# Moving delta*u*B of a selective scan from VectorE to ScalarE and TensorE, one state at a time

## Chip, core and metric

The kernel runs on one core of a Trainium2 chip. The metric is the device time of one launch in microseconds (us). Before the change it is 28022.95 us, the median of three runs (27987.81 to 28037.46). The core has five engines that run side by side, each with its own queue of instructions: TensorE (PE, matmuls and transposes, with its weight loads shown apart as PEld), VectorE (DVE), ScalarE (ACT), GpSimd (POOL) and SyncE (SP, which issues most DMAs). PE's results go to PSUM, a small memory from which DVE and ACT read; everything else lies in the large on-chip memory, SBUF. [...]

## What is computed

An image batch of four 128x128 images with 128 channels goes through two residual layers, each after a group norm. Layer 0 is a deformable convolution: offsets from a 3x3 convolution, a bilinear gather at nine taps, a depthwise and a pointwise convolution. Layer 1 treats each image row, 128 pixels, as a sequence of tokens t, and runs two Mamba blocks over it. The part that the change touches is the selective scan of a block:

```
delta  = softplus(dt @ dtw + dtb)
deltaA = exp(delta[t,d] * A[d,n])
deltaBu = (delta * u)[t,d] * B[t,n]
h = deltaA * h + deltaBu          # along t, for each channel d and state n
y[t,d] = sum_n h[t,d,n] * C[t,n] + u * D
out = (y * silu(res)) @ ow
```

There are 256 channels d (`NC` = 2 chunks of 128 partitions), 16 states n (`NS`), and two blocks (`NL`). Everything is fp32.

## The kernel before, in words

Work of layer 1 comes in jobs. A job is one block `l` of one group of `SR` = 4 image rows, 512 tokens (`TB`); there are 128 groups and two blocks, so 256 jobs. A job has two parts. `pre` (lines 484 to 551) makes what the scan needs, with channels on the partitions and tokens along the free axis: u (`pu` matmuls, L501, then silu, L508), the gate g (L513, L518), the small projection `dbl` with dt, B and C (L521, L524), delta (`pdt` matmuls L534, the softplus as Abs, Exp, Identity, Ln on ACT, L538 to L546, and the joins on DVE, L547 to L549), and du = delta*u (L550). B and C are written to DRAM (`bcd`, L526), so that they can be read back with every partition holding the same row.

`main` (lines 553 to 631) goes over the states in rounds of `NQ` = 2. In a round, SP loads the two B rows and the two C rows, each spread over 128 partitions (L570). ACT sets the first column of every row in the decay tile to zero (L575), so that one long scan restarts at each row, and writes the decays exp(delta*A) beside it (L580), into one of `NDA` = 3 fixed tiles `da`. DVE multiplies du by B into `hs` (L584), scans over 2048 elements in one instruction with the result in `da` (L591), and multiplies by C (L595). PE then transposes the sixteen 128x128 blocks and adds them in the two PSUM banks of `y` (`add_transposed`, L128, called at L603), where the sum over n is made. At the end of a job the result is gated (L606), transposed back (L611), projected (L616, L623, L625) and either becomes the next block's input h or goes out.

Layer 0 of an image: POOL gathers table entries with indirect DMAs (L364) into the four `gt` buffers, DVE weighs them (`gw`, L382), PE transposes them into `p` (L128 again), ACT copies that out (L396), and PE makes the convolution sums `acc` (L415). `prep` computes locations and weights eight rows ahead.

Layer 1 of image b and layer 0 of image b+1 are written interleaved, by counting: one step of layer 0 (a unit of eight gathers) after a share of a round of layer 1 (the loop at lines 656 to 669). In the program, `pre` of the next job is written before `main` of the present one. The order on each engine is not that of the program text, though: a scheduler of the framework places instructions by its own estimate of when each is ready, with earlier text first among those that are ready, and adds the semaphores. A tile's tag has a number of buffers (`bufs`); a new tile of a tag waits until the last user of the oldest one is done.

Four pools share PSUM before the change: `ps` (layer 0's transposes and small matmuls, 2 buffers of a bank), `psa` (`acc`, 2), `ps1` (everything in `pre` and at the end of a job, 2) and `psy` (`y`, one buffer of two banks).

Of the kernel before, what the change touches and what calls it, by code (L numbers as in the profile page):

```python
# [10 lines left out]
F32 = mybir.dt.float32  # L11
# [6 lines left out]
P = 128  # L18
# [45 lines left out]
def block_kernel(ctx: ExitStack, tc: tile.TileContext, a: dict, out: bass.AP):  # L64
# [27 lines left out]
    ps = ctx.enter_context(tc.tile_pool(name="l0ps", bufs=2, space=PSUM))  # L92
# [3 lines left out]
    ps1 = ctx.enter_context(tc.tile_pool(name="l1ps", bufs=2, space=PSUM))  # L96
# [29 lines left out]
    def add_transposed(o, v, start, stop):  # L126

        nc.tensor.matmul(o, v, ident, is_transpose=True, start=start, stop=stop, skip_group_check=True)  # L128
# [355 lines left out]
    def pre(st, l):  # L484
# [40 lines left out]
        bcd = pd.tile([2 * NS, TB], F32, tag="bcd", name=f"bcd_{nm}")  # L525
        nc.sync.dma_start(bcd, dbl[DTR + 1 : XP, :])  # L526
# [3 lines left out]
        du = p2.tile([P, NC, TB], F32, tag="du", name=f"du_{nm}", bufs=2)  # L530
# [20 lines left out]
        st.update(u=u, g=g, delta=de, du=du, bcd=bcd)  # L551

    def main(st, l):
# [11 lines left out]
        for q in range(NS // NQ):  # L565
            bc = []
            for w in range(2):
                t = p2.tile([P, NQ, TB], F32, tag=f"bc{w}", name=f"bc{w}_{nm}_{q}", bufs=2)
                n0 = w * NS + q * NQ
                nc.sync.dma_start(t, st["bcd"][n0 : n0 + NQ, :].partition_broadcast(P))  # L570
                bc.append(t)
            da = das[n_da[0] % NDA]
            n_da[0] += 1

            nc.scalar.copy(da.rearrange("p c n s t -> p (c n s) t")[:, :, 0], zero)  # L575
            for c in range(NC):
                dv = st["delta"][:, c].rearrange("p (s t) -> p s t", s=SR)
                for n in range(NQ):
                    s = q * NQ + n
                    nc.scalar.activation(  # L580
                        da[:, c, n, :, 1:], dv[:, :, 1:], AF.Exp, scale=aneg[:, l, c, s : s + 1]
                    )
            hs = p2.tile([P, NC, NQ, TB], F32, tag="hs", name=f"hs_{nm}_{q}")
            nc.vector.tensor_tensor(  # L584
                hs,
                st["du"].unsqueeze(2).to_broadcast([P, NC, NQ, TB]),
                bc[0].unsqueeze(1).to_broadcast([P, NC, NQ, TB]),
                ALU.mult,
            )
            df = da.rearrange("p c n s t -> p (c n s t)")  # L590
            nc.vector.tensor_tensor_scan(  # L591
                df, df, hs.rearrange("p c n t -> p (c n t)"), 0.0, ALU.mult, ALU.add
            )
            dc = da.rearrange("p c n s t -> p c (n s t)")
            nc.vector.tensor_tensor(  # L595
                dc, dc,
                bc[1].rearrange("p n t -> p (n t)").unsqueeze(1).to_broadcast([P, NC, NQ * TB]),
                ALU.mult,
            )
            for c in range(NC):  # L600
                for n in range(NQ):
# [145 lines left out]
```

## Time and profile before

| | |
|---|---|
| median of three runs | 28022.95 us |
| the profiled execution, its own time | 28027.08 us |
| its span | 28025.3 us |
| mean granted PE clock | 0.834 |
| DVE busy | 22925.4 us |
| PE busy | 19874.5 us |
| POOL busy | 18817.1 us |
| ACT busy | 11640.4 us |
| moved by DMA | 3804.39 MB, 136 GB/s |

The page of a profile gives the busy time of each engine, a strip of the span in slices, and groups of instructions: line, engine, operation, output and inputs, count, busy time, the mean of one in ns, and how long the engine stood idle just before them with what ended that idle time. Windows give the same busy times for a stretch of the span. The timeline lists instructions with their start and duration in us. A wait is put down to what came last. Busy time of PE is modelled and somewhat too long for matmuls that follow one another closely, since these overlap; the distance from start to start is the better measure there.

### The profile page before, as it was taken

Reading aid. Unit: us, or ns where it says so; the run is one execution under the profiler, and the core shown is the slowest. Engines: PE = TensorE matmul, PEld = TensorE weight load, DVE = VectorE, ACT = ScalarE, POOL = GpSimd, SP = SyncE. Lnnn points to the kernel's source line nnn. Section 1 sums busy time; section 2 is a strip of 40 time slices with the busy share of each in tenths; the row PEclk is TensorE's granted clock in tenths of the full one; section 3 lists DMA queues with packets and bytes.
Section 4 is the critical chain, followed back from the end, with each engine's and each line's share of the span. In section 5 each row is a group of like instructions: output and inputs, shape, how many; then the busy total and the mean of one; then the engine's idle time right before and its main releaser. Section 6 shows DMA issues by size and latency. Waiting matters only on the chain. (4 is left out here: it accounts for less than half of the span.)

```text
span 28025.3 us, 292712 instructions
## 1 busy us (share of the span) xinstructions
PE 19874.5 (71%) x112196; PEld 13790.6 (49%) x112196; DVE 22925.4 (82%) x11994; ACT 11640.4 (42%) x18190; POOL 18817.1 (67%) x9222
## 2 busy tenths in 40 slices
PE   4777777777777777777777777777777755555555
PEld 3444455555555545555555555555555544434344
DVE  2232288888888898888888898888888899999999
ACT  0000144444444444444444444444444455555554
POOL 4777788888888878888888878888888800000000
PEclk7888888888888888888888888888888877667777
DMA  5363344455444444445444444444444433333333
GB/s 142 114 168 107 111 142 145 146 161 162 149 142 139 142 135 146 147 151 168 152 142 144 139 138 140 144 142 144 140 143 143 138 113 107 109 107 109 107 109 104
DMA packets 1994584, 3804.39 MB, mean 136 GB/s; under 512 B 771795, under 2 KB 1116115, under 8 KB 1993052
## 3 DMA queue, kind: packets, MB, share of 16 engines
q1 hardware_dynamic: 1550812, 2577.13, 28.6%
q0 software_dynamic: 442368, 1208.55, 13.6%
q8 instruction: 880, 14.42, 0.2%
q14 instruction: 524, 4.29, 0.0%
HBM read 3567.63 MB, written 217.05 MB: 135 GB/s over the span
## 5 line engine op out<-in xcount | busy, mean ns | idle before, releaser
L364 POOL DMA_INDIRECT gt<-table,idx x9216 | 18816.4, 2042 | 3674.8 <-issue 3042.2
L591 DVE TENSOR_TENSOR_SCAN da<-da,hs 128x2048 f32<-128x2048 f32 x2048 | 9056.4, 4422 | 498.9 <-ACT da L580 407.2
L128 PE MATMUL y<-ident,da 128*128 128x128 f32 x32768 | 5361.3, 331 | 4518.1 <-DVE da L595 4515.5
L580 ACT ACTIVATE da<-de,aneg 128x508 f32<-128x508 f32 x8192 | 5569.7, 713 | 6349.2 <-PE y L128 6151.5
L128 PEld LDWEIGHTS y<-ident,da 128*128 128x128 f32 x32768 | 4780.2, 174 | 5499.1 <-DVE da L595 3050.8
L415 PE MATMUL acc<-s,wc 128*64 128x256 f32 (+3 forms) x38400 | 6435.8, 457 | 887.3 <-ACT s L396 885.9
L382 DVE TENSOR_TENSOR gw<-gt,wt 128x1024 f32<-128x1024 f32 x2304 | 2794.9, 1219 | 3919.9 <-DMA gt<-table,idx 3268.9
L415 PEld LDWEIGHTS acc<-s,wc 128*64 128x64 f32 x38400 | 3399.3, 147 | 3237.7 <-issue 1456.8
L595 DVE TENSOR_TENSOR da<-da,bc 128x2048 f32<-128x2048 f32 x2048 | 4688.0, 2289 | 25.5
L584 DVE TENSOR_TENSOR hs<-du,bc 128x2048 f32<-128x2048 f32 x2048 | 4680.3, 2285 | 0.0
L128 PE MATMUL p<-ident,gw 128*128 128x128 f32 x18432 | 2790.5, 304 | 2015.4 <-DVE gw L382 2007.3
L128 PEld LDWEIGHTS p<-ident,gw 128*128 128x128 f32 x18432 | 2361.0, 158 | 2609.6 <-DVE gw L382 2036.7
L396 ACT COPY s<-p 128x512 f32<-128x512 f32 x1152 | 669.8, 582 | 4377.9 <-PE p L128 4370.7
L501 PE MATMUL pu<-hp,inc 128*128 128x512 f32 x4096 | 1808.3, 593 | 0.0
L580 ACT ACT_TABLE_LOAD x1019 | 1307.4, 1283 | 10.2
L501 PEld LDWEIGHTS pu<-hp,inc 128*128 128x128 f32 x4096 | 751.9, 189 | 865.1 <-issue 864.9
L508 ACT ACTIVATE u<-pu,w_cvb 128x512 f32<-128x512 f32 x512 | 324.0, 683 | 1448.5 <-PE y L561 1442.5
L611 PE MATMUL pyg<-ident,g 128*128 128x128 f32 x2048 | 366.0, 337 | 522.0 <-DVE g L606 521.9
L561 PEld LDWEIGHTS y<-ddiag,u 128*128 128x128 f32 x4096 | 585.1, 202 | 197.6 <-issue 197.6
L546 ACT ACT_TABLE_LOAD x506 | 649.2, 1283 | 9.0
L612 ACT COPY yg<-pyg 128x512 f32<-128x512 f32 x512 | 284.9, 588 | 813.3 <-PE pyg L611 813.2
L561 PE MATMUL y<-ddiag,u 128*128 128x128 f32 x4096 | 614.4, 285 | 0.0
(118 smaller groups left out, 11438.6 us busy)
## 6 DMA issues: line engine op xcount, KB each, us to landing
bc<-bcd SPq DMA_DIRECT2D x4096, 512.0 KB
gt<-table,idx POOLq DMA_INDIRECT x9216
table<-xt SPq DMA_DIRECT2D x984, 128.0 KB
xt<-in_x SPq DMA_DIRECT2D x124, 320.0 KB
xr<-in_x SPq DMA_DIRECT2D x128, 256.0 KB
x<-xo SPq DMA_DIRECT2D x128, 256.0 KB
x1t<-x SPq DMA_DIRECT2D x128, 256.0 KB
x1t_o<-x SPq DMA_DIRECT2D x128, 256.0 KB
```

Of the source, the lines that this page charges most:

```text
L128: nc.tensor.matmul(o, v, ident, is_transpose=True, start=start, stop=stop, skip_group_check=True)
L364: nc.gpsimd.indirect_dma_start(out=gt[:, v, r], out_offset=None, in_=flat, in_offset=bass.IndirectOffsetOnAxis(ap=idx[:, ri, o : o + 1], a ...
L382: nc.vector.tensor_tensor(gw.rearrange("p r s v c -> p (r s) v c"), gts[h].rearrange("p v r (s c) -> p (r s) v c", c=CG), wv.unsqueeze(3). ...
L396: nc.scalar.copy(st[:, :, 1 : W + 1], p4)
L415: nc.tensor.matmul(accs[b, j + i0][CG * g : CG * g + CG, q : q + rb - ra, :], wc[sl, v, e, :], st[p + 4 * g if p < 4 else 8][sl, ra:rb, kx ...
L501: nc.tensor.matmul(px.rearrange("p (s t) -> p s t", s=SR), inc[:, l, j, c * P : (c + 1) * P], h[:, :, j : j + P], start=(j == 0), stop=(j ...
L546: nc.scalar.activation(du[:, c], w1, AF.Ln)
L561: nc.tensor.matmul(y[:, i, c], st["u"][:, c, i * P : (i + 1) * P], ddiag[:, l, c, :], start=(i % 2 == 0 and c == 0), stop=False, skip_grou ...
L580: nc.scalar.activation(da[:, c, n, :, 1:], dv[:, :, 1:], AF.Exp, scale=aneg[:, l, c, s : s + 1])
L584: nc.vector.tensor_tensor(hs, st["du"].unsqueeze(2).to_broadcast([P, NC, NQ, TB]), bc[0].unsqueeze(1).to_broadcast([P, NC, NQ, TB]), ALU.mult,
L591: nc.vector.tensor_tensor_scan(df, df, hs.rearrange("p c n t -> p (c n t)"), 0.0, ALU.mult, ALU.add)
L595: nc.vector.tensor_tensor(dc, dc, bc[1].rearrange("p n t -> p (n t)").unsqueeze(1).to_broadcast([P, NC, NQ * TB]), ALU.mult,)
```

## The change

delta*u*B is no longer made by DVE. At the end of `pre`, PE transposes du into `ps1`, and ACT copies it to `dut`, with tokens on the partitions and channels along the free axis. B is transposed in the same way into `bt`, tokens on the partitions, one column for each state. For each state, ACT then multiplies: four copies of 128x256, one for each image row, with the state's column of `bt` as the scale that differs by partition, into `xs`. PE transposes the eight 128x128 blocks of `xs` into `px`, two PSUM banks, and the scan reads its second input there.

`main` now goes one state at a time: scans, products with C and decays cover 1024 elements for each instruction, not 2048. The decays keep three tiles, now half as large, of their own: the scan writes to `hs` (three buffers), so the zeros in the first columns are set once at the start and stay, and the copy of L575 is gone. Only C goes through DRAM (`cd`), two rows at a time into `cs`. The sixteen transposes for `y` of two states are as before.

To make room in PSUM, `ps` and `ps1` go from two buffers to one, and `psx` (px) takes two banks. `du` has one buffer where it had two. The load of `cvw` during set-up is split into one for each block.

```diff
-    ps = ctx.enter_context(tc.tile_pool(name="l0ps", bufs=2, space=PSUM))
+    ps = ctx.enter_context(tc.tile_pool(name="l0ps", bufs=1, space=PSUM))
...
-    ps1 = ctx.enter_context(tc.tile_pool(name="l1ps", bufs=2, space=PSUM))
+    ps1 = ctx.enter_context(tc.tile_pool(name="l1ps", bufs=1, space=PSUM))
+    psx = ctx.enter_context(tc.tile_pool(name="l1psx", bufs=1, space=PSUM))
...
-    cvw = loadw("cvw", [P, NL, DCONV, NC * P], pool=p2, tag="hs")
     for l in range(NL):
+        cvw = p2.tile([P, DCONV, NC * P], F32, tag="dut", name=f"w_cvw_{l}", bufs=2)
+        nc.sync.dma_start(cvw, a["cvw"][:, l])
...
-    das = [cw.tile([P, NC, NQ, SR, P], F32, name=f"da{i}") for i in range(NDA)]
-    zero = cw.tile([P, NC * NQ * SR], F32, name="zero")
-    nc.vector.memset(zero, 0.0)
+    das = [cw.tile([P, NC, SR, P], F32, name=f"da{i}") for i in range(NDA)]
+    for t in das:
+        nc.vector.memset(t, 0.0)
...
-        bcd = pd.tile([2 * NS, TB], F32, tag="bcd", name=f"bcd_{nm}")
-        nc.sync.dma_start(bcd, dbl[DTR + 1 : XP, :])
+        cd = pd.tile([NS, TB], F32, tag="cd", name=f"cd_{nm}")
+        nc.sync.dma_start(cd, dbl[DTR + 1 + NS : XP, :])
+
+        pbt = ps1.tile([P, SR, XP], F32, tag="t", name=f"pbt_{nm}")
+        for i in range(SR):
+            nc.tensor.transpose(pbt[:, i, :], dbl[:, i * P : (i + 1) * P], ident[0:XP, 0:XP])
+        bt = p2.tile([P, SR, NS], F32, tag="bt", name=f"bt_{nm}", bufs=2)
+        nc.scalar.copy(bt, pbt[:, :, DTR + 1 : DTR + 1 + NS])
...
-        du = p2.tile([P, NC, TB], F32, tag="du", name=f"du_{nm}", bufs=2)
+        du = p2.tile([P, NC, TB], F32, tag="du", name=f"du_{nm}")
...
+        dut = p2.tile([P, SR, NC * P], F32, tag="dut", name=f"dut_{nm}", bufs=2)
+        for k in range(SR // 2):
+            pt = ps1.tile([P, 2, NC, P], F32, tag="t", name=f"pdu_{nm}_{k}")
+            for i in range(2):
+                for c in range(NC):
+                    o = (2 * k + i) * P
+                    nc.tensor.transpose(pt[:, i, c, :], du[:, c, o : o + P], ident)
+            nc.scalar.copy(dut[:, 2 * k : 2 * k + 2], pt.rearrange("p s c d -> p s (c d)"))
...
-        for q in range(NS // NQ):
...
+        for n in range(NS):
+            if n % NQ == 0:
+                cs = p2.tile([P, NQ, TB], F32, tag="cs", name=f"cs_{nm}_{n}", bufs=2)
+                nc.sync.dma_start(cs, st["cd"][n : n + NQ, :].partition_broadcast(P))
             da = das[n_da[0] % NDA]
             n_da[0] += 1
-
-            nc.scalar.copy(da.rearrange("p c n s t -> p (c n s) t")[:, :, 0], zero)
             for c in range(NC):
                 dv = st["delta"][:, c].rearrange("p (s t) -> p s t", s=SR)
...
+                nc.scalar.activation(da[:, c, :, 1:], dv[:, :, 1:], AF.Exp, scale=aneg[:, l, c, n : n + 1])
+
+            xs = p2.tile([P, SR, NC * P], F32, tag="xs", name=f"xs_{nm}_{n}", bufs=2)
+            for i in range(SR):
+                nc.scalar.activation(xs[:, i], st["dut"][:, i], AF.Copy, scale=st["bt"][:, i, n : n + 1])
+            px = psx.tile([P, NC, SR, P], F32, tag="x", name=f"px_{nm}_{n}")
+            for c in range(NC):
+                for i in range(SR):
+                    nc.tensor.transpose(px[:, c, i, :], xs[:, i, c * P : (c + 1) * P], ident)
+            hs = p2.tile([P, NC, TB], F32, tag="hs", name=f"hs_{nm}_{n}", bufs=3)
+            nc.vector.tensor_tensor_scan(
+                hs.rearrange("p c t -> p (c t)"),
+                da.rearrange("p c s t -> p (c s t)"),
+                px.rearrange("p c s t -> p (c s t)"),
+                0.0, ALU.mult, ALU.add,
+            )
             nc.vector.tensor_tensor(
-                hs,
-                st["du"].unsqueeze(2).to_broadcast([P, NC, NQ, TB]),
-                bc[0].unsqueeze(1).to_broadcast([P, NC, NQ, TB]),
-                ALU.mult,
-            )
...
+                hs, hs, cs[:, n % NQ].unsqueeze(1).to_broadcast([P, NC, TB]), ALU.mult
             )
             for c in range(NC):
-                for n in range(NQ):
-                    for i in range(SR):
-                        add_transposed(y[:, i, c], da[:, c, n, i, :], False, q == NS // NQ - 1 and n == NQ - 1)
-            yield
+                for i in range(SR):
+                    add_transposed(y[:, i, c], hs[:, c, i * P : (i + 1) * P], False, n == NS - 1)
+            if n % NQ == NQ - 1:
+                yield
```

More of the change, by code (lines that the diff above doesn't have):

```diff
@@ L162, in block_kernel @@
     inw = loadw("inw", [P, NL, NC * P], a["inw"][:, :, 0 : NC * P], pool=p2, tag="yg")
-    cvw = loadw("cvw", [P, NL, DCONV, NC * P], pool=p2, tag="hs")
     for l in range(NL):
+        cvw = p2.tile([P, DCONV, NC * P], F32, tag="dut", name=f"w_cvw_{l}", bufs=2)
+        nc.sync.dma_start(cvw, a["cvw"][:, l])
         nc.vector.tensor_tensor(
-            inc[:, l], cvw[:, l], inw[:, l].unsqueeze(1).to_broadcast([P, DCONV, NC * P]), ALU.mult
+            inc[:, l], cvw, inw[:, l].unsqueeze(1).to_broadcast([P, DCONV, NC * P]), ALU.mult
         )
@@ L550, in pre @@
         nc.vector.tensor_tensor(du, de, u, ALU.mult)
-        st.update(u=u, g=g, delta=de, du=du, bcd=bcd)
+        dut = p2.tile([P, SR, NC * P], F32, tag="dut", name=f"dut_{nm}", bufs=2)
[6 more added lines that the diff above has]
+            nc.scalar.copy(dut[:, 2 * k : 2 * k + 2], pt.rearrange("p s c d -> p s (c d)"))
+        st.update(u=u, g=g, delta=de, dut=dut, bt=bt, cd=cd)
     def main(st, l):
@@ L564, in main @@
                 )
-        for q in range(NS // NQ):
[L566 to L571, printed above, removed]
+        for n in range(NS):
+            if n % NQ == 0:
+                cs = p2.tile([P, NQ, TB], F32, tag="cs", name=f"cs_{nm}_{n}", bufs=2)
+                nc.sync.dma_start(cs, st["cd"][n : n + NQ, :].partition_broadcast(P))
@@ L572, in main @@
             da = das[n_da[0] % NDA]
             n_da[0] += 1
-            nc.scalar.copy(da.rearrange("p c n s t -> p (c n s) t")[:, :, 0], zero)
             for c in range(NC):
                 dv = st["delta"][:, c].rearrange("p (s t) -> p s t", s=SR)
-                for n in range(NQ):
-                    s = q * NQ + n
-                    nc.scalar.activation(
-                        da[:, c, n, :, 1:], dv[:, :, 1:], AF.Exp, scale=aneg[:, l, c, s : s + 1]
-                    )
-            hs = p2.tile([P, NC, NQ, TB], F32, tag="hs", name=f"hs_{nm}_{q}")
@@ L584, in main @@
-            nc.vector.tensor_tensor(
-                hs,
-                st["du"].unsqueeze(2).to_broadcast([P, NC, NQ, TB]),
-                bc[0].unsqueeze(1).to_broadcast([P, NC, NQ, TB]),
-                ALU.mult,
[L589 to L598, printed above, removed]
+                nc.scalar.activation(da[:, c, :, 1:], dv[:, :, 1:], AF.Exp, scale=aneg[:, l, c, n : n + 1])
+            xs = p2.tile([P, SR, NC * P], F32, tag="xs", name=f"xs_{nm}_{n}", bufs=2)
+            for i in range(SR):
+                nc.scalar.activation(xs[:, i], st["dut"][:, i], AF.Copy, scale=st["bt"][:, i, n : n + 1])
@@ L599, in main @@
+            nc.vector.tensor_tensor(
+                hs, hs, cs[:, n % NQ].unsqueeze(1).to_broadcast([P, NC, TB]), ALU.mult
             )
             for c in range(NC):
-                for n in range(NQ):
-                    for i in range(SR):
-                        add_transposed(y[:, i, c], da[:, c, n, i, :], False, q == NS // NQ - 1 and n == NQ - 1)
-            yield
+                for i in range(SR):
+                    add_transposed(y[:, i, c], hs[:, c, i * P : (i + 1) * P], False, n == NS - 1)
```

## The prediction

> **What bounds the kernel now.** I read the page's first parts, then cut the span where layer 1's first decay (L580) starts, 3475 us, and where the last gather (L364) starts, 22487 us. The page, then the windows, one stage per line (busy us and counts of PE, PEld, DVE, ACT, POOL; granted clock; DMA share):
> ```profile
> span 28025.3 us, 292712 instructions
> PE 19874.5 (71%) x112196; PEld 13790.6 (49%) x112196; DVE 22925.4 (82%) x11994; ACT 11640.4 (42%) x18190; POOL 18817.1 (67%) x9222
> ...
> 0.00:3475.00 3475.00, 2542.32 (x15688) 1549.81 (x15689) 979.16 (x1163) 259.57 (x455) 2431.39 (x2342) 0.86 0.46 128
> 3475.00:22487.00 19012.00, 14409.03 (x83109) 9992.62 (x83108) 16767.24 (x8738) 8549.34 (x13422) 16380.25 (x6881) 0.87 0.45 145
> 22487.00:28025.00 5538.00, 2923.11 (x13400) 2248.13 (x13400) 5179.03 (x2095) 2831.53 (x4314) 5.50 (x1) 0.71 0.31 108
> ```
> Stage A is layer 0 alone, B both layers, C layer 1 alone. The whole share (DVE 82%) hides three limits. In C DVE is busy 94%. In B, POOL's 16380 us and the 2024 us of issue gaps that its own line shows there make 97%: B is POOL's. The groups say on what:
> ```profile
> L364 POOL DMA_INDIRECT gt<-table,idx x9216 | 18816.4, 2042 | 3674.8 <-issue 3042.2 <-DVE gw L382 552.8 <-DMA gt<-table,idx 39.6
> L591 DVE TENSOR_TENSOR_SCAN da<-da,hs 128x2048 f32<-128x2048 f32 x2048 | 9056.4, 4422 | 498.9 <-ACT da L580 407.2 <-DVE hs L584 3.8
> L580 ACT ACTIVATE da<-de,aneg 128x508 f32<-128x508 f32 x8192 | 5569.7, 713 | 6349.2 <-PE y L128 6151.5 <-DVE hs L584 35.5 <-DVE gw L382 3.2
> L595 DVE TENSOR_TENSOR da<-da,bc 128x2048 f32<-128x2048 f32 x2048 | 4688.0, 2289 | 25.5
> L584 DVE TENSOR_TENSOR hs<-du,bc 128x2048 f32<-128x2048 f32 x2048 | 4680.3, 2285 | 0.0
> ```
> L584's idle is 0.0: it never waits for its broadcast rows. ACT's 6151 us is waiting for a free `da`: slack, not cost. Then one line of POOL's gathers in a piece of A (800 to 3400 us), then in B (6000 to 22000); durations are least, median, most:
> ```profile
> L364 POOL DMA_INDIRECT gt<-table,idx x1934: 942/946/2255, 800.3 to 3400.0; - x194
> ...
> L364 POOL DMA_INDIRECT gt<-table,idx x5787: 942/1899/13837, 6000.3 to 21999.9; - x200
> ```
> The same gather takes twice as long beside layer 1. The timeline (start, duration) shows why: three gathers while DVE is idle until 24.46, the next beside the scan:
> ```profile
> 10022.75 0.94 POOL L364 DMA_INDIRECT gt<-table,idx  x1 [0.30 <-issue]
> 10023.99 0.94 POOL L364 DMA_INDIRECT gt<-table,idx  x1 [0.30 <-issue]
> 10025.24 4.40 POOL L364 DMA_INDIRECT gt<-table,idx  x1 [0.31 <-issue]
> ...
> 10024.46 4.42 DVE L591 TENSOR_TENSOR_SCAN da<-da,hs 128x2048 f32<-128x2048 f32 x1 [4.08 <-ACT da L580]
> ```
> In C a round of two states is scan, times C, next du*B, and PE comes after:
> ```profile
> 25044.99 2.29 DVE L595 TENSOR_TENSOR da<-da,bc 128x2048 f32<-128x2048 f32 x1
> 25047.20 2.29 DVE L584 TENSOR_TENSOR hs<-du,bc 128x2048 f32<-128x2048 f32 x1
> 25047.43 3.65 PE L128 MATMUL y<-ident,da 128*128 128x128 f32 x16 [6.58 <-DVE da L595]
> 25049.62 4.42 DVE L591 TENSOR_TENSOR_SCAN da<-da,hs 128x2048 f32<-128x2048 f32 x1
> ```
> Scan to scan is 9.09 us (25040.53 to 25049.62), all DVE. B holds 1509 such rounds, C 539 (the scans in each), so a job (block and layer, 8 rounds) costs 19012/188.6 = 100.8 us in B and 5538/67.4 = 82.2 in C.
>
> [...] Sixteen transposes take 3.65 us in C and 1.91 at 10031.86 us[...]
>
> **The change part by part, for a round of two states.**
> DVE: L584 goes, -2.29. One scan of 2048 becomes two of 1024. A 1024 TENSOR_TENSOR is 1.215 (L550), a 2048 one 2.289: 1.07 per 1024 and 0.14 fixed; with that fixed part a half scan is 0.14+4.28/2 = 2.28. [...] Times C: 2x1.215 for 2.289. Net -2.29+0.14+0.14 = -2.0.
> ACT: the zero copy goes (-0.21: nothing overwrites the decays any more, so column 0 stays zero). Eight 128x256 copies with a per-partition scale come. Runs of four L580 take 2.54, 0.635 each for 508[...]. +3.4, or +4.0. In C that is 2832-113+1833 us = 4.55 ms, and two 0.59 us copies of du's transposes and one of about 0.4 of B's a job add 0.11: 4.66. Where decays slip between the two silus of u or of g, which one ps1 bank pulls apart, up to four more table loads of 1.28 a job come (1.3 ms over 256 jobs); they may stay away, so they are in the range, not in the sum.
> PE: 16 more transposes a round, 1.8 warm or 3.4 cold, and 12 a job.
> SP: L570's 4096 issues of 512 KB become 2048; B no longer goes through DRAM. Worth 0, because DMA was not waited for; if C's rows came late, the C product would wait, and y's transposes after it. One more set-up load hides in A, before layer 1.
> POOL: scans read one SBUF input, so gathers stay blocked only by the C product, `gw` and the small products. Between 0.95+0.30 and today's 2.38+0.30 each; I take about 1.6 in all, 11 ms in B: POOL stops being the limit. If it does not, B stays.
>
> New floors in B: DVE 16767-1509x2.0 = 13.7 ms. ACT 8549-315+1509x3.4+0.3 = 13.7. PE 14409+1509x1.8+0.25 = 17.4 at today's clock of 0.87, or 14409x0.87+2.97 = 15.5 all warm. PE takes over. In C: DVE 4.1, ACT 4.66, PE 3.9 to 5.0.
>
> Waits. px has one buffer: scan n must end before PE fills px for n+1, and scan n+1 waits for that. From the rows: 0.12 handover (25047.28 to 25047.40), eight transposes about 1.05 warm or 2.0 cold, 0.12 back: 1.3 or 2.2, with the C product (1.2) beside it. A state takes 2.28+1.3 = 3.6 warm, 4.5 cold; a round 7.2 to 9.0 against 9.09. In B, px queues on PE behind layer 0's matmuls; the scan waits, and behind it on DVE the `gw` products, which release `gt` and so POOL's next gathers. A px that waits for its scan holds up, on PE, `p`, `acc` and `pre`'s matmuls. ps1 with one bank makes `pre` serial: it took 38.7 us at 24999.47 (first pu to L550's end), 47.6 at 9999.67. Now pdt_1 waits until L548 has read pdt_0 (+9), pu and pr lose their overlap (+4), transposes of B and du follow (+4.5): 56 and 65, plus about 9 from L606 to the new h. That is 65 and 74, inside 16 states. ps with one bank: A's unit is eight gathers, 9.9 us, against 1.9 PE + 0.6 ACT: nothing.
>
> Sum: A 3475. B: PE between 15.5 and 17.4, middle 16.4. PE answers three engines in order, so it will not reach POOL's 97%; I choose 90%, between that and its own 76% of today: 18.2 ms, 96.5 a job. C: 67.4 jobs of 58 (warm) to 72 (cold), 4 to 10 at job ends, ACT's 69: 75, so 5.05 ms. Total 26.7 ms. The profiled execution took 28027 us, 2 above its span and 4 above the median, so no correction.
>
> **Rivals.**
> 1. Better: POOL freed and PE warm throughout. B at 15.5/0.93 = 16.7, C at 70 a job 4.7: 24.9 ms. For it: the clock already averages 0.87. Against: layer 0's blocks sit between px and scan.
> 2. Slower: the single ps1 bank makes `pre` the bound. It decides once the chain exceeds 100.8 us in B and 82.2 in C. From 74 and 65, some 25 handovers each need 1.1 and 0.7 us more. ACT, rising from 45% to about 75% busy in B, can do that. At 105 and 86: 19.8+5.8+3.5 = 29.1 ms. Against: ACT idles 6 ms today.
> 3. Order: y's transposes of state n stand before px of n+1 on PE. A state is then 2.28+1.2+1.0+1.3+0.24 = 6.0 warm, 7.9 cold; at 6.5, 16 states are 104; with job ends 114 in B and 108 in C: 21.5+7.3+3.5 = 32 ms. Against: PE's order in the trace follows readiness (L513 cuts into y's transposes), and px is ready before the C product ends.
> 4. No gain: gathers stay at 2.4, C cold: 28.0.
>
> **How the numbers follow.** Forecast 0.43 (own range 25.6 to 27.9 ms), rival 1 0.12, 2 0.32, 3 0.09, 4 0.04. Faster 0.55, same 0.04, slower 0.41; 0.2% is about what a measurement here can tell. Below 24.6 lies some 0.05, above 30.2 0.14 (rival 3 and the worst of 2), so 24.6 to 30.2 ms.
>
> **What would show it.** Gathers in B near 1.3 us median; half scans near 2.28; px's copies near 0.43; DVE waiting for PE px, 0.1 to 1.0 us a state; PE busy over 85% in B at a higher clock. Wrong: DVE waiting 5 us or more for the first px of a job (rival 2), or px starting after y (rival 3).

## The result: slower by 5.7%

With the change the launch takes 29611.51 us (median of four runs, 29596.76 to 29616.73) against 28021.02 us before (four runs, 27987.81 to 28037.46). The ratio is 1.0568, 95% interval 1.055 to 1.0587. The forecast was 26.7 ms, faster: wrong in sign, by 2.9 ms, though the time lies inside the range. The profiled execution took 29596.76 us.

The start of the changed kernel's page:

```profile
span 29595.0 us, 380164 instructions
PE 24029.2 (81%) x148036; PEld 16438.4 (56%) x148036; DVE 18882.7 (64%) x14044; ACT 18740.4 (63%) x33595; POOL 10665.6 (36%) x9222
```

The windows over the same three stages (A 0 to 3432, B to 23427, C to the end; columns as before: PE, PEld, DVE, ACT, POOL busy us and counts, granted clock, DMA share, GB/s):

```profile
0.00:3432.00 3432.00, 2446.93 (x15763) 1610.58 (x15763) 987.70 (x1168) 265.63 (x457) 2391.33 (x2348) 0.86 0.46 130
3432.00:23427.00 19995.00, 17274.13 (x109112) 11649.65 (x109113) 13683.79 (x10217) 13687.06 (x24635) 8273.61 (x6875) 0.97 0.32 98
23427.00:29595.00 6168.00, 4308.10 (x23162) 3178.18 (x23161) 4211.23 (x2660) 4787.71 (x8504) 0.70 (x1) 0.85 0.15 52
```

A is as before. B grew by 1.0 ms, although DVE's work in it fell from 16.8 to 13.7 ms and POOL's from 16.4 to 8.3. C grew by 0.6 ms, although DVE's fell from 5.2 to 4.2. Counting scans, B holds 188.0 jobs and C 68.0, so a job costs 106.4 us in B (100.8 before) and 90.7 in C (82.2). In B PE is the busiest engine, 86% of the time. In C no engine is near its limit: ACT, the busiest, has 78%.

The groups say what DVE does with the freed time (busy, mean ns, then the idle time just before and what ended it):

```profile
L366 POOL DMA_INDIRECT gt<-table,idx x9216 | 10664.9, 1157 | 12761.4 <-DVE gw L384 9851.3
L600 DVE TENSOR_TENSOR_SCAN hs<-da,px 128x1024 f32<-128x1024 f32 x4096 | 9353.8, 2284 | 6595.2 <-PE px L598 6038.4
L594 ACT ACTIVATE xs<-dut,bt 128x256 f32<-128x256 f32 x16384 | 7149.9, 496 | 1584.0 <-PE px L598 1576.7
L598 PE MATMUL px<-ident,xs 128*128 128x128 f32 x32768 | 5043.2, 294 | 3523.3 <-DVE hs L600 3320.5
```

The scan stands idle for 6595 us where the old one had 499. It waits for px, px waits for the scan before it, ACT's copies wait for px. POOL no longer issues gather after gather: it waits 9851 us for `gw`, which is behind the scan on DVE. Idle time of DVE for each job, summed over the trace: in B 33.6 us (11.9 before), 25.2 of it ahead of scans; in C 28.6 (5.2), 27.3 of it ahead of scans. DVE's work fell by 16.1 and 14.9 us a job, its idle time rose by 21.7 and 23.4.

The gathers became fast, as forecast; one line for them in B (least, median, most ns):

```profile
L366 POOL DMA_INDIRECT gt<-table,idx x5465: 940/947/4628, 5999.8 to 21999.8; - x196
```

And a state without `pre` in its way costs in C what was forecast, 3.6 us (timeline: start, duration, engine, line):

```profile
27033.58 2.29 DVE L600 TENSOR_TENSOR_SCAN hs<-da,px 128x1024 f32<-128x1024 f32 x1
27035.91 1.23 DVE L606 TENSOR_TENSOR hs<-hs,cs 128x1024 f32<-128x1024 f32 x1
27036.02 1.07 PE L598 MATMUL px<-ident,xs 128*128 128x128 f32 x8 [1.34 <-DVE hs L600]
27037.19 1.09 PE L129 MATMUL y<-ident,hs 128*128 128x128 f32 x8
27037.19 2.29 DVE L600 TENSOR_TENSOR_SCAN hs<-da,px 128x1024 f32<-128x1024 f32 x1
```

Scan to scan is 3.61 us: the scan ends at 35.87, px starts at 36.02, takes eight transposes, and the next scan starts at 37.19. Here px passes in front of y. Thirty microseconds earlier, while PE, ACT and DVE also work on the next job's `pre`, the same eight transposes are cut in three:

```profile
27003.83 0.87 PE L598 MATMUL px<-ident,xs 128*128 128x128 f32 x3 [2.54 <-DVE hs L600]
27005.00 1.97 PE L129 MATMUL y<-ident,hs 128*128 128x128 f32 x8 [0.30 <-DVE hs L606]
27006.76 0.78 PE L598 MATMUL px<-ident,xs 128*128 128x128 f32 x4
27007.47 1.12 PE L542 MATMUL pdt<-dbl,w_dtw 9*128 9x512 f32 x2
27008.53 0.33 PE L598 MATMUL px<-ident,xs 128*128 128x128 f32 x1
27008.89 2.29 DVE L600 TENSOR_TENSOR_SCAN hs<-da,px 128x1024 f32<-128x1024 f32 x1 [2.62 <-PE px L598]
```

From the first transpose to the scan 5.1 us instead of 1.2. In B it is layer 0 that comes between:

```profile
12042.61 1.21 DVE L606 TENSOR_TENSOR hs<-hs,cs 128x1024 f32<-128x1024 f32 x1
12043.88 1.09 PE L129 MATMUL y<-ident,hs 128*128 128x128 f32 x8 [0.61 <-DVE hs L606]
12044.90 3.65 PE L417 MATMUL acc<-s,wc 128*64 128x384 f32 x18
12048.48 1.09 PE L598 MATMUL px<-ident,xs 128*128 128x128 f32 x8
12049.68 2.29 DVE L600 TENSOR_TENSOR_SCAN hs<-da,px 128x1024 f32<-128x1024 f32 x1 [5.86 <-PE px L598]
```

PE is busy all the time from 43.88 to 49.57, but the one thing that DVE needs comes last; DVE stands for 5.86 us.

### The profile page after: what moved, and what is told of

It reads as the page before. It is cut to its first block, busy times and chain, and to the rows that moved or that the text cites. A ratio compares the mean times of both kernels' runs of the same rounds, so it can differ in the third digit from the quotient of the medians.

```text
span 29595.0 us, 380164 instructions
## 1 busy us (share of the span) xinstructions
PE 24029.2 (81%) x148036; PEld 16438.4 (56%) x148036; DVE 18882.7 (64%) x14044; ACT 18740.4 (63%) x33595; POOL 10665.6 (36%) x9222
## 3 DMA queue, kind: packets, MB, share of 16 engines
q1 hardware_dynamic: 1251948, 1494.87, 16.1%
## 4 chain that ended last, share of the span: by engine, by line
issue 34%; DVE 21%; PE 20%; POOL 19%; DMA 3%; ACT 3%; SPq 1%; DVEq 0%; POOLq 0%; ACTq 0%
POOL gt L366 19%; DVE hs L600 13%; PE px L598 4%; DVE hs L606 4%; PE acc L417 4%; PE y L129 4%; PE pu L503 3%; DMA gt<-table,idx 2%; DVE gw L384 2%; PE pdt L542 1%; ACT xs L594 1%; PE pdb L523 1%; ACT da L590 1%; PE y L578 1%; PE pr L515 1%
## 5 line engine op out<-in xcount | busy, mean ns | idle before, releaser
L366 POOL DMA_INDIRECT gt<-table,idx x9216 | 10664.9, 1157 | 12761.4 <-DVE gw L384 9851.3
L600 DVE TENSOR_TENSOR_SCAN hs<-da,px 128x1024 f32<-128x1024 f32 x4096 | 9353.8, 2284 | 6595.2 <-PE px L598 6038.4
L594 ACT ACTIVATE xs<-dut,bt 128x256 f32<-128x256 f32 x16384 | 7149.9, 496 | 1584.0 <-PE px L598 1576.7
L598 PE MATMUL px<-ident,xs 128*128 128x128 f32 x32768 | 5043.2, 294 | 3523.3 <-DVE hs L600 3320.5
L598 PEld LDWEIGHTS px<-ident,xs 128*128 128x128 f32 x32768 | 3889.6, 149 | 5050.1 <-ACT xs L594 1790.7
L129 PE MATMUL y<-ident,hs 128*128 128x128 f32 x32768 | 4910.0, 294 | 744.0 <-DVE hs L606 682.0
L129 PEld LDWEIGHTS y<-ident,hs 128*128 128x128 f32 x32768 | 3948.8, 151 | 2245.8 <-DVE hs L606 1568.5
L606 DVE TENSOR_TENSOR hs<-hs,cs 128x1024 f32<-128x1024 f32 x4096 | 5003.8, 1222 | 68.3
L129 PEld LDWEIGHTS p<-ident,gw 128*128 128x128 f32 x18432 | 2202.1, 148 | 1085.6 <-issue 557.1
L542 PE MATMUL pdt<-dbl,w_dtw 9*128 9x512 f32 x1024 | 653.2, 721 | 2.5 <-DVE de L556 1.8
```

Of the source, the lines that this page charges most:

```text
L366: nc.gpsimd.indirect_dma_start(out=gt[:, v, r], out_offset=None, in_=flat, in_offset=bass.IndirectOffsetOnAxis(ap=idx[:, ri, o : o + 1], a ...
L542: nc.tensor.matmul(pdt, dtw[:, l, c * P : (c + 1) * P], dbl[0 : DTR + 1, :], start=True, stop=True)
L594: nc.scalar.activation(xs[:, i], st["dut"][:, i], AF.Copy, scale=st["bt"][:, i, n : n + 1])
L598: nc.tensor.transpose(px[:, c, i, :], xs[:, i, c * P : (c + 1) * P], ident)
L600: nc.vector.tensor_tensor_scan(hs.rearrange("p c t -> p (c t)"), da.rearrange("p c s t -> p (c s t)"), px.rearrange("p c s t -> p (c s t)" ...
L606: nc.vector.tensor_tensor(hs, hs, cs[:, n % NQ].unsqueeze(1).to_broadcast([P, NC, TB]), ALU.mult)
```

## The theories

Four readings of this, which the experiments tell apart:

- **O, order:** px has one buffer, so it cannot be filled ahead of time, and when it may be filled it stands behind other work on PE. DVE waits for it.
- **P, load:** PE simply has 15.5 us more to do for each job (91.9 busy in B against 76.4). Whatever the order, B cannot be much shorter.
- **K, bank:** ps1 has one bank (a single buffer, for tiles of up to 128x512 fp32 in the program), which makes `pre` serial. This is the prediction's rival 2; its time, 29.1 ms, is the nearest to what came.
- **L, lead:** ACT is too little ahead with decays and `xs`.

For L the trace of the changed kernel itself is nearly enough. Taking for each scan its start, the end of the decays and copies that it needs, and px's start and end: of DVE's idle time ahead of scans in B (4732 us), `xs` was unfinished in 26 us; px had its `xs` and had not begun in 2861; px was running in 1749. In C (1854 us) these are 107, 352 and 1318. The decays were never late. In all this idle time PE did, in B, mostly `acc` (1314 us), `pu` (946), y (740) and px itself (674), and in C y (522), px (493) and `pu` (383). L is out as a cause of the waits.

All ratios below are to the kernel before, run in turn on the same chip. In two of the comparisons (e5b to e10) stage A took some 0.8 ms longer in every kernel that was profiled (4.1 to 4.3 ms), and the kernel before took 28.6 and 28.8 ms, not 28.0; why is not known. So between experiments B and C are compared, in us a job.

## Experiments

**K: one bank each, in the kernel before** (e1_single_banks).

```diff
-    ps = ctx.enter_context(tc.tile_pool(name="l0ps", bufs=2, space=PSUM))
+    ps = ctx.enter_context(tc.tile_pool(name="l0ps", bufs=1, space=PSUM))
-    ps1 = ctx.enter_context(tc.tile_pool(name="l1ps", bufs=2, space=PSUM))
+    ps1 = ctx.enter_context(tc.tile_pool(name="l1ps", bufs=1, space=PSUM))
```

> The kernel before with only the two PSUM pools cut: ps and ps1 from two buffers to one; the scan as before. Theory O (PE's order: px has one buffer and stands behind other PE work, and DVE waits for it): nothing of that loop is here, so within 1% of before, 27.8 to 28.3 ms. Theory K (rival 2: the single ps1 bank makes pre serial and pre becomes the bound): most of the loss is here, 29 ms or more.

27484.62 us against 27973.19, ratio 0.9822 (0.9806 to 0.9839): 1.8% less, which neither theory had expected. The scan's group on its page, and the window of C:

```profile
L591 DVE TENSOR_TENSOR_SCAN da<-da,hs 128x2048 f32<-128x2048 f32 x2048 | 9050.4, 4419 | 102.3 <-ACT da L580 14.7
...
22228.00:27502.00 5274.00, 3084.61 (x13500) 2296.55 (x13500) 5187.91 (x2105) 3165.24 (x4611) 4.21 (x2) 0.72 0.33 114
```

Before, the scan waited 499 us, 407 of it for decays. C falls from 82.2 to 78.0 a job, and DVE's idle time ahead of scans there from 4.9 to 0.6; B falls from 100.8 to 99.7. So the single banks by themselves do not cost time: in the kernel before they gain. They gain although ACT loads its function tables 11.2 times a job in B and 11.8 in C, against 8.0 and 7.9 (1.28 us each); that is ACT's time, which had slack. Why the decays come sooner is only argued: a `pre` that must wait for its bank takes fewer of ACT's turns ahead of the current scan.

**K: ps1 not alone, in the changed kernel** (e3_shared_banks). Both users share two banks.

```diff
-    ps = ctx.enter_context(tc.tile_pool(name="l0ps", bufs=1, space=PSUM))
+    ps = ctx.enter_context(tc.tile_pool(name="l0ps", bufs=2, space=PSUM))
-    ps1 = ctx.enter_context(tc.tile_pool(name="l1ps", bufs=1, space=PSUM))
+    ps1 = ps
```

> The changed kernel with ps and ps1 drawn from one pool of two banks, so that pre has both banks to itself once layer 0 is over. Theory K: a job of the last stage falls from 90 us to 80 or less, the total to 28.9 ms or less. Theory O: that stage stays within 3%, the total between 29.2 and 29.8 ms.

29743.75 us, ratio 1.0635 (1.0617 to 1.0653): no better than the change. Its windows:

```profile
3471.00:23986.00 20515.00, 17454.64 (x109237) 12311.79 (x109238) 13708.78 (x10224) 12867.24 (x24026) 7863.16 (x6887) 0.93 0.31 96
23986.00:29745.30 5759.30, 4103.44 (x23158) 3073.01 (x23156) 4194.79 (x2660) 4333.16 (x8170) 1.18 (x2) 0.88 0.16 55
```

C did fall, 90.7 to 84.7, more than theory O allowed and less than K asked for, while B rose, 106.4 to 109.1. Table loads fell from 9.9 to 5.0 a job in C, which is 6.3 us of ACT's time, about the size of C's gain. So in C some of the loss can be `pre` being cut up by its one bank, though through table loads and not through the chain of rival 2; in B sharing with layer 0 only hurts. A `ps1` with two banks of its own was not tried beside px. Yet two kernels below (e4, e10) keep both single banks and all of `pre`'s new transposes, and B falls to 87.2 and 88.8 us a job. So K is refuted as the cause of B's loss, and as the main one of C's.

**O: px in halves that can be filled ahead** (e2_px_halves). Two one-bank halves with a buffer each, two scans of 512 for each state: while one half is scanned, the other can be filled.

```diff
-    psx = ctx.enter_context(tc.tile_pool(name="l1psx", bufs=1, space=PSUM))
+    psx = ctx.enter_context(tc.tile_pool(name="l1psx", bufs=2, space=PSUM))
...
+            for c in range(NC):
+                px = psx.tile([P, SR, P], F32, tag="x", name=f"px_{nm}_{n}_{c}")
+                for i in range(SR):
+                    nc.tensor.transpose(px[:, i, :], xs[:, i, c * P : (c + 1) * P], ident)
+                nc.vector.tensor_tensor_scan(
+                    hs[:, c], da[:, c].rearrange("p s t -> p (s t)"),
+                    px.rearrange("p s t -> p (s t)"), 0.0, ALU.mult, ALU.add,
+                )
```

> The changed kernel with px as two one-bank halves and one scan of 512 for each half, so that PE can fill one half while DVE scans the other. DVE does 4096 more scans at 0.14 us of fixed cost, 0.57 ms more. Theory O: DVE's 6.0 ms of waiting for px falls by half or more, 27.0 to 28.5 ms. Theory K: pre's chain is untouched, 29.6 to 30.2 ms.

28364.65 us, ratio 1.0141 (1.0124 to 1.0158). That wins back 4.3 of the 5.7%, with DVE's busy time a little up (72.8 to 73.3 us a job in B). Windows of B and C:

```profile
3443.00:22868.00 19425.00, 17371.58 (x109138) 11525.21 (x109139) 13777.14 (x13227) 13769.35 (x24648) 8288.46 (x6873) 0.98 0.32 101
22868.00:28381.40 5513.40, 4219.40 (x23138) 2925.78 (x23136) 4216.00 (x3747) 4726.41 (x8504) 0.95 (x1) 0.89 0.17 58
```

C falls by 9.6 us a job (to 81.1) and B by 3.1 (to 103.3), with PE busy 89% of B. The wait is real. In C undoing part of it gains much, in B little: there 3975 us of DVE's waiting for px are left of 4462.

**O without P: transposes that nobody reads** (e5b_px_unread). A half p0 is filled at the start of a job and all scans read it; px is still transposed, into a bank of its own that no scan reads. The true delta\*u\*B is left out of the scan.

```diff
+            if n == 0:
+                p0 = psx.tile([P, SR, P], F32, tag="x", name=f"p0_{nm}")
+                for i in range(SR):
+                    nc.tensor.transpose(p0[:, i, :], xs[:, i, 0:P], ident)
             for c in range(NC):
+                px = psx.tile([P, SR, P], F32, tag="xj", name=f"px_{nm}_{n}_{c}")
...
+                nc.vector.tensor_tensor_scan(
+                    hs[:, c], da[:, c].rearrange("p s t -> p (s t)"),
+                    p0.rearrange("p s t -> p (s t)"), 0.0, ALU.mult, ALU.add,
+                )
```

> The kernel with px halves, but the scans read one half filled at the start of the job (the values of the other states are left out of the result); PE still makes all transposes of xs, into a bank that nobody reads. PE, ACT and DVE do the same work as with halves, only DVE does not wait for px and PE does not wait for the scan. Theory O (the waiting in the loop costs): 25.5 to 26.8 ms. Theory P (PE's load costs, the wait is only where it shows): 27.8 ms or more.

28490.5 us against 28802.77, ratio 0.9892 (0.9876 to 0.9909).

```profile
4284.00:23541.00 19257.00, 16868.95 (x109875) 11997.03 (x109876) 13826.31 (x13226) 13649.60 (x24661) 8198.74 (x6871) 0.96 0.33 102
23541.00:28492.80 4951.80, 4101.08 (x23422) 2918.66 (x23421) 4218.42 (x3747) 4524.75 (x8372) 0.59 (x1) 0.89 0.19 64
```

C is 72.8 a job, 17.9 less than with the change, with ACT busy 91% of it. B is 102.4: taking DVE's wait for px away brings 4.0, only 0.9 more than the halves. DVE's idle time in B is nearly the same (28.8 a job, 30.0 with the halves). Part of it has moved, to the softplus joins (5.4) and the gate (4.8); 13.6 still stands ahead of scans. PE's queue is still waited for, as two lines of its waits show (us in the whole run, times, longest):

```profile
DVE hs L605 <- PE p L598: 1213.9, 132, 26.8
...
ACT xs L594 <- PE px L602: 1174.5, 632, 9.4
```

DVE waits for p0, once a job, and ACT for the transposes that release its two `xs` tiles. In B alone the two are 1086 and 1143 us, 5.8 and 6.1 a job.

**P: px once a job, and not at all** (e4_px_once, e10_no_px). In the first, px is filled at state 0 and read by all sixteen scans. The second is the kernel of the unread px with those transposes taken out. ACT makes all copies `xs` in both; delta\*u\*B of the other states (of all but p0's, in the second) is left out of the result.

```diff
-            px = psx.tile([P, NC, SR, P], F32, tag="x", name=f"px_{nm}_{n}")
-            for c in range(NC):
+            if n == 0:
+                px = psx.tile([P, NC, SR, P], F32, tag="x", name=f"px_{nm}_{n}")
+                for c in range(NC):
...
-            for c in range(NC):
-                px = psx.tile([P, SR, P], F32, tag="xj", name=f"px_{nm}_{n}_{c}")
-                for i in range(SR):
-                    nc.tensor.transpose(px[:, i, :], xs[:, i, c * P : (c + 1) * P], ident)
```

> The changed kernel with px filled for the first state of a job only; the other 15 scans read the same px (their values are left out of the result), ACT still makes every xs. Theory O: DVE no longer waits for PE in the loop and PE loses 30720 transposes; B falls to 15.5 to 16.5 ms, C to about 4.9, total 24 to 25.5 ms. Theory K: jobs stay at what pre's chain takes, total 28 ms or more. A third theory (L: ACT, with two xs tiles and three decay tiles, is too little ahead) also gives 28 ms or more.

> As the kernel with px's transposes into a bank that nobody reads (102.4 us a job in B, 72.8 in C), but these transposes are left out altogether; the scans read halves filled once a job, so du*B is left out of the result. ACT still makes xs. Nobody waits for px in either. If PE's load is what holds B, B falls by PE's 14.6 us a job, to 86 to 90. If the wait or ACT's copies held it, B stays within 3 us of 102. C: ACT about 66 us busy a job, so 69 to 72.8.

Once a job: 25363.77 us, ratio 0.9069 (0.9054 to 0.9085). Not at all: 26477.51 against 28627.17, ratio 0.9248 (0.9228 to 0.9269). Windows of B and C, first for once a job, then for not at all:

```profile
3435.00:19850.00 16415.00, 14122.25 (x86637) 9408.62 (x86638) 13565.79 (x10224) 14203.54 (x25117) 8092.35 (x6872) 0.94 0.39 120
19850.00:25366.00 5516.00, 3539.99 (x14917) 2456.39 (x14915) 4123.40 (x2653) 4766.32 (x8526) 1.28 (x2) 0.68 0.17 57
...
4225.00:20951.00 16726.00, 14101.68 (x85911) 9359.84 (x85912) 13708.59 (x13243) 14290.57 (x25112) 8726.89 (x6872) 0.94 0.39 117
20951.00:26488.30 5537.30, 3489.48 (x14619) 2374.68 (x14617) 4177.02 (x3732) 4853.61 (x8576) 1.28 (x1) 0.68 0.17 57
```

B is 87.2 a job in the first and 88.8 in the second, both as expected. Between the unread px and none, DVE waits for px in neither; PE's busy time in B falls by 14.8 us a job (89.7 to 74.9) and B by 13.6 (102.4 to 88.8). That is P, almost one for one. It is the load with what hangs on it: DVE's wait for p0 falls to 179 us in B, and ACT's wait for `xs` to be released goes with the transposes. These runs do not part the two. ACT's own load is not what holds B at 102: it rose a little, to 75.9.

In C both were a miss: 81.4 a job, where 4.9 ms or some 72 was expected, and 81.8, with 69 to 72.8 expected. Against the unread px, less work took 9 us more. Two things differ. ACT has 5.2 us more in the second (71.7 against 66.5), nearly all of it table loads (11.9 against 7.9 a job, at 1.28): by the trace decays stand between the silus of `pre`, and each such switch loads a table (in the changed kernel's trace all 1242 between a silu and a decay, either way). The scans of C wait 749 us for decays, where the unread px had 402. But PE's granted clock in C is 0.68, not 0.89, too, and the 144 transposes for y of a job take 28.7 us instead of 18.8. ACT's time is the likelier cause, since it is busy 88% of C and PE 63%, but no run separates the two.

**One state at a time, du\*B by DVE** (e6b_one_state, then e8_one_state_single_banks with `ps` and `ps1` at one buffer). Both leave ACT and PE alone: DVE multiplies into an SBUF tile `xs` of 1024, two buffers, and the scan reads that; scan, C product, decays and `hs` as in the change.

```diff
+            xs = p2.tile([P, NC, TB], F32, tag="xs", name=f"xs_{nm}_{n}", bufs=2)
+            nc.vector.tensor_tensor(
+                xs, st["du"], bs[:, n % NQ].unsqueeze(1).to_broadcast([P, NC, TB]), ALU.mult
+            )
```

> Only the part one state at a time: decays, du*B, scan and C product of 1024, three decay tiles of their own, the zero column set once; du*B still by DVE, B through DRAM, PSUM pools of two as before. DVE pays 2x0.14 for the halved scan and products and one more product's 0.14, 0.42 us a round, 0.86 ms in all, ACT saves the zero copies. From that 28.3 to 29.2 ms. If the shorter lead of the decays (three states, not six) costs by itself, 29.5 ms or more.

> The kernel before, one state at a time, du*B by DVE in SBUF, with ps and ps1 at one buffer each: the two edits that paid by themselves (ratios 0.972 and 0.982) put together. If they act on different things, the ratio is near 0.972 x 0.982 = 0.955, some 26.75 ms against 28.0. If both only relieve the same thing (the order in which PE serves pre, p and y), the ratio stays at 0.97. DVE per job in B about 90 us as before, gathers near 1.9 us mean.

27981.94 us against 28802.77, ratio 0.9721 (0.9705 to 0.9737): a gain where a loss was expected. With it the gathers' mean is 1875 ns, 2042 before, and DVE's idle time ahead of `gw` in B falls from 10.2 to 3.2 us a job. With single banks 27663.45 us against 28627.17, ratio 0.9666 (0.965 to 0.9683). The two edits add up only in part; their product would be 0.955. By its ratio to the kernel before, the second is the fastest kernel of this study, those that leave work out aside. Its windows:

```profile
4205.00:22350.00 18145.00, 14296.25 (x82975) 9741.83 (x82974) 16936.06 (x13253) 9243.88 (x12509) 14929.91 (x6871) 0.88 0.49 152
22350.00:27597.90 5247.90, 3100.82 (x13479) 2204.74 (x13476) 5208.68 (x3723) 3109.60 (x4065) 1.83 (x1) 0.71 0.34 114
```

B is 96.3 a job with DVE busy 93% of it, C 77.7 with DVE busy 99%. This kernel has the changed one's pools for `ps` and `ps1`, its state-by-state loop and its three decay tiles; what differs is who makes delta\*u\*B, and the single buffer of du that goes with it. So the path through ACT, PE and PSUM costs 10.1 us a job in B (96.3 to 106.4) and 13.0 in C, 188 x 10.1 + 68 x 13.0 = 2.8 ms. These jobs were timed on two chips; by the ratios, each taken on one chip, it is 1.0568 less 0.9666, 9.0% or 2.5 ms. The rest of the change gains 1.0 ms (3.3%).

**DVE writes the product into PSUM** (e9_product_in_psum): as the last, but `xs` is a tile of two banks with one buffer.

```diff
-            xs = p2.tile([P, NC, TB], F32, tag="xs", name=f"xs_{nm}_{n}", bufs=2)
+            xs = psx.tile([P, NC, TB], F32, tag="x", name=f"xs_{nm}_{n}")
```

> As the run before it, but DVE writes du*B into two PSUM banks and the scan reads its second input there. DVE's work is the same, ACT and PE get nothing more. If what relieved the gathers was that the scan has one SBUF input, their mean in B falls from about 1.9 to near 1.2 us, POOL stops being the limit there, and B goes down to DVE's own 90 us with some idle, 93 to 95 a job against about 95 to 97: ratio 0.93 to 0.95. If DVE pays for the PSUM access, its scans or products rise above 2.28 and 1.22 us. In C the single buffer costs nothing, since the writer and the reader are the same engine: the same time a job as in the run before it, within 1 us.

27894.0 us against 28627.17, ratio 0.9739 (0.9723 to 0.9756). The gathers were as expected; the window of B follows them:

```profile
L366 POOL DMA_INDIRECT gt<-table,idx x9216 | 11899.8, 1291 | 10359.4 <-DVE gw L384 7320.7 <-issue 2923.6 <-DVE hs L584 49.6
...
4205.00:22258.00 18053.00, 14635.71 (x82815) 9339.23 (x82813) 17173.86 (x13225) 9402.35 (x12623) 9477.62 (x6871) 0.91 0.49 153
```

Their mean is 1291 ns, 1883 in the kernel with SBUF, and POOL now waits for `gw`. B did not profit: 96.1 against 96.3, with 93 to 95 expected. DVE is busy 95% of B (93% with SBUF), so relieving POOL could bring little. C was a miss: 83.0, not 77.7. DVE's timeline there:

```profile
25020.64 2.29 DVE L584 TENSOR_TENSOR_SCAN hs<-da,xs 128x1024 f32<-128x1024 f32 x1
25022.96 1.23 DVE L588 TENSOR_TENSOR hs<-hs,cs 128x1024 f32<-128x1024 f32 x1
25024.10 1.22 DVE L580 TENSOR_TENSOR xs<-du,bs 128x1024 f32<-128x1024 f32 x1
25025.46 2.29 DVE L584 TENSOR_TENSOR_SCAN hs<-da,xs 128x1024 f32<-128x1024 f32 x1
```

With SBUF and two buffers, two states run in pairs, in an order in which no instruction reads what the one before it has just written:

```profile
25048.29 4.47 DVE L583 TENSOR_TENSOR_SCAN hs<-da,xs 128x1024 f32<-128x1024 f32 x2 [0.77 <-ACT hp L493]
25052.67 2.34 DVE L587 TENSOR_TENSOR hs<-hs,cs 128x1024 f32<-128x1024 f32 x2
25054.93 2.35 DVE L579 TENSOR_TENSOR xs<-du,bs 128x1024 f32<-128x1024 f32 x2
25057.20 4.47 DVE L583 TENSOR_TENSOR_SCAN hs<-da,xs 128x1024 f32<-128x1024 f32 x2
```

One buffer forces 4.82 us a state (25020.64 to 25025.46); pairs take 4.46 ((25057.20 - 25048.29)/2). The instructions are hardly longer. But a product whose scan follows directly starts 1.36 us ahead of it (24.10 to 25.46), products in the pairs 1.13; and a scan starts 2.32 ahead of the C product that reads it, in the pairs 2.19. Sixteen times 0.36 is 5.8; C lost 5.3. Most of this goes with the order and not with PSUM: in the kernel before, where all of it lies in SBUF, the scan starts 2.42 after the product that it reads (25047.20 to 25049.62 in the prediction's lines), while a product that does not read the one before it starts 2.21 after it (25044.99 to 25047.20).

**Only some states through px** (e7b_every_second; e11_every_fourth, and e12_fourth_rest_psum with the other products in px's banks). Pools as in the change, but `xs` has one buffer instead of two and du two instead of one. The diff is that of every second state; for every fourth the test is n % 4 == 0, and in the last kernel the product goes to a tile of `psx`, not to `hs`.

```diff
+            if n % 2 == 0:
+                xs = p2.tile([P, SR, NC * P], F32, tag="xs", name=f"xs_{nm}_{n}", bufs=1)
...
+                src = px.rearrange("p c s t -> p (c s t)")
+            else:
+                nc.vector.tensor_tensor(hs, st["du"], bs.unsqueeze(1).to_broadcast([P, NC, TB]), ALU.mult)
+                src = hs.rearrange("p c t -> p (c t)")
```

> The changed kernel with only the even states made by ACT and PE; for the odd ones DVE multiplies du by B into hs, as before, and scans from there. PE has a DVE product, two scans and two C products to fill px in, about 7 us, not 1.2. DVE does 8.2 us a round, between 7.0 of the change and 9.0 of before. Theory O: DVE's wait for px is nearly gone, 25.5 to 27.2 ms, below both kernels. Theory P or a bound of ACT: 27.8 ms or more.

> One state in four goes through xs and px as in the change, the other three have du*B made by DVE in SBUF; pools as in the change. Against all sixteen by DVE with single banks (96.3 us a job in B, 77.7 in C, ratio 0.967): DVE loses four products, -4.9 us; PE gets 32 transposes of px and twelve more a job, about +4.8. If a state through px costs DVE a wait of 1.3 to 1.6 us (25.2 us for sixteen with the change, 10.7 for eight with every second state), the four bring 5 to 6 us back: B 96 to 98, ratio 0.965 to 0.98. If the wait only comes when PE is over 85% busy, B is 91 to 92 and C 73 to 75: ratio 0.92 to 0.93. If what spoilt every second state (107.8) lies elsewhere, B is above 100.

> As the run before it, but the other three products go by DVE into the two banks of px, so that every scan has only one SBUF input and the gathers are not held up by it: gathers near 1.3 us mean (against 1.8 to 1.9). DVE alone bounded that form (91.4 of 96.1 us a job in B, 80.0 of 83.0 in C); with four products less it has 86.5 and 75. If the px wait comes back as above, B is 96 to 98; if not, B is 90 to 92, and this is the fastest kernel of all, ratio 0.91 to 0.93.

Every second state: 30131.15 us against 28802.77, ratio 1.0467 (1.045 to 1.0485), a plain miss: B 107.8, C 82.1. Every fourth: 27181.41 against 27993.63, ratio 0.971 (0.9693 to 0.9726), B 98.8, C 76.3. Every fourth with the rest in PSUM: 27204.78, ratio 0.9718 (0.9701 to 0.9734), B 96.0, C 84.1. Windows of B of these three, in this order:

```profile
4250.00:24545.00 20295.00, 16341.01 (x97209) 11239.69 (x97210) 15306.27 (x11733) 11206.06 (x18534) 10550.89 (x6871) 0.91 0.38 117
```

```profile
3440.00:22038.00 18598.00, 15210.74 (x91222) 10365.66 (x91222) 16125.09 (x12488) 10214.07 (x15692) 12762.33 (x6872) 0.91 0.44 138
```

```profile
3441.00:21490.00 18049.00, 15366.84 (x91093) 9912.30 (x91093) 16292.54 (x12471) 10424.22 (x15862) 9215.02 (x6875) 0.94 0.45 142
```

The last is the clean pair to the product in PSUM (e9): DVE's busy time in B falls by 4.7 us a job (91.4 to 86.7), as it should, and its idle time rises by 4.7 (4.7 to 9.4), that ahead of scans from 1.0 to 5.9. B is the same, 96.1 and 96.0. The waits of the whole run put 1376 us on px, 1.3 for each of the 1024 states that go through it (with the change 6038.4 over 4096, 1.5), against 1.2 us of DVE work saved. Without the PSUM product, against e8, DVE's busy time in B fell by 4.2 and its idle time grew by 6.7: 3.4 of it ahead of products, which wait for y's transposes to free `hs`, and 2.0 ahead of the joins; ahead of scans it is 1.5, less than e8's 2.2. So here it is not the wait for px that takes the gain back. Every second state has 10.7 a job ahead of its eight px scans, and besides 6.7 ahead of the joins and 6.0 ahead of `gw`; no engine is busy over 81% of its B. Why it comes out above both its neighbours is not settled; its single `xs` tile was not tested apart.

## Why the prediction was wrong

**Right, term by term.** DVE in B 13.7 ms (13.68), half scans 2.28 us (2.284 with px in PSUM, 2.276 in e8 with both inputs in SBUF); ACT in B 13.7 (13.69); `xs` copies, 0.425 us each by the author's estimate, start 0.425 apart (four in 1.70 where they run unhindered). ACT in C 4.66 (4.79; two more table loads a job are 0.17). Gathers blocked by less, by what the last section measures: 1.20 us mean and 0.30 of gap in B, where 1.6 in all was taken; POOL is no limit any more. Broadcast rows and set-up load cost nothing: A is 3432. A state undisturbed is 3.6 us (3.61). PE becomes the busiest engine of B.

**Failed: PE's sum in B, in two terms.** The sum put PE in B between 15.5 and 17.4 ms and took the middle, 16.4, because the granted clock would rise. The clock rose, from 0.87 to 0.97, and PE's busy time still came out at 17.27 ms: 91.9 us a job, 4.9 above the middle. The middle held 5.0 us a job of gain on PE's old work (71.4 for 76.4), got by multiplying that work by the clock. What the prediction calls warm and cold are two granted clocks in the trace of before: sixteen transposes took 1.91 us at 1.00 (10031.86) and 3.65 at 0.50 (25047.43). That all of PE's busy time would shrink in step with the mean granted clock was the author's estimate. In the changed kernel's trace the old work takes 72.7 to 75.0 us a job. (Matmul records overlap, by 0.07 us at 12048.48: the first figure counts a shared moment to the matmul that began first, the second always to the old work.) So 1.4 to 3.7 of the 5.0 came. The new transposes take the rest, 16.9 to 19.2, where 15.7 was priced (8 rounds of 1.8, and 1.3): 1.8 belongs to sixteen in a row (0.109 from start to start at 10031.86, 1.91 in all), but px comes in eights, and eight take 1.07 where nothing disturbs them (27036.02), 2.1 a round. The prediction itself had 1.05 for eight, among its waits.

Then the share of B in which PE is busy: 90% was chosen, 86% came. 17.27/0.90 for 16.4/0.90 is +1.0 ms, 86.4% for 90% another +0.8. The mechanism, PE's load, was right in the main (with px off PE, B is 87.2 in e4 and 88.8 in e10); with its size right, the sum would have ended at 27.7 ms with the chosen share, and at 28.5 with the true one, even if C had come as forecast. The forecast of faster hung on these two terms.

**Failed: C's 75 us a job.** 75 was made of sixteen states with nothing ahead of px on PE, warm or cold (58 to 72), and 4 to 10 for the ends of jobs. The undisturbed state exists, but only late in a job: by position in the job, the mean distance of scans in C is 8.0, 9.8, 6.3, 4.5, 5.8, 7.8, 7.2, 5.7 us for the first eight and 3.6 only from the twelfth to the fourteenth. In the others the next job's `pre` is on PE between scan and px. The prediction named this queue for layer 0 in B, and priced it nowhere; in C it was taken as free. What it is worth depends on the kernel that one takes for comparison: with the wait for px gone from the loop C is 72.8 in e5b, 17.9 less and close to the 75, but 81.4 in e4 and 81.8 in e10, where PE's clock is lower and ACT loads its tables more often (10.9 and 11.9 times a job for 7.9). So the wait is worth some 9 to 18 us a job, and its exact share stays open. C came out at 6.17 ms instead of 5.05. Together: 26.7 + 1.0 + 0.8 + 1.1 = 29.6.

**The rivals.** Rival 2 gave 29.1 ms, the nearest time, with a wrong mechanism, so that is luck: its single bank gains time in the kernel before (e1), and undoing it does not help (e3), apart from C's table loads. Its test, five microseconds or more of waiting for the first px of a job, held in 60 jobs of B and one of C. The longest waits came at a job's third state (8.5 us on the mean in B, 6.3 in C), with px behind or between other work on PE. Rival 3, y ahead of px, holds in part and not as a rule: of DVE's idle time ahead of scans PE spent 740 of 4732 us on y in B, and in C 522 of 1854, there more than on anything else. Rivals 1 and 4 failed, the one on PE's load, the other on the gathers.

**What was not weighed.** DVE's product was traded for a round trip DVE, PE, DVE of 1.3 us at best, of which the product with C hides most. Undisturbed that is a gain: 3.61 us a state, against 9.09/2 = 4.5 before and 4.46 in e8. But those 0.85 us are all there is to win on a state, and the new state waits for whatever else stands on PE; the one of e8 needs no handover for its product.

## What to carry to other kernels

Work taken from a busy engine is not yet a gain if the new path has a handover in the inner loop. Here a producer on another engine with a single buffer between gave back more than was saved: in B DVE's work fell by 16.1 us a job and its idle time rose by 21.7. The loss depends on what else that engine serves. Price such a wait by what stands in the other engine's queue in each stage, not by the undisturbed loop. Price the new work in the pieces in which the loop issues it, and where a busy engine gets more work, count on no gain from a higher clock until a run shows it.

## What was not expected of the hardware

- PE's granted clock rose from 0.87 to 0.97 in B, and its busy time for the same work fell only from 76.4 to between 72.7 and 75.0 us a job. In step with the clock it would have been 68.5, an estimate from these figures (76.4 x 0.87/0.97).
- One PSUM bank in place of two, in two pools, made the kernel before 1.8% faster; why is only argued.
- Gathers take 1883 ns on the mean when the scan beside them reads two SBUF tiles (e8) and 1291 when one of them is in PSUM (e9; medians in B 1880 and 947); the pair differs in this operand, and in one buffer for two. In the traces of before and after, the time of a gather in B goes by the DVE instruction during which it starts. Before, the median is 4.16 us inside the scan of two SBUF tiles (1089 gathers). After, it is 0.946 inside the scan that reads px (2173 gathers, the longest 0.957), 0.946 inside the product that gates y in PSUM (139), but 1.69 inside the C product (1278) and 1.65 inside `gw` (878), which read two SBUF tiles.
- Two DVE products of 1024 that do not read each other start 1.13 us apart though each lasts 1.21; a scan that reads the product ahead of it starts 1.36 after it (product in PSUM). With the order that one buffer forces, C took 5.3 us a job more.
